# Output additions at later places, the layout transposes split by batch, and a prelude that starts its statistics two places later

## The chip, the cores and the metric

The kernel runs on one core of one Trainium2 chip. The metric is the device time of one execution in microseconds, as the median of several runs. TensorE is called PE here, its weight loads PEld, VectorE DVE, ScalarE ACT, GpSimd POOL and SyncE SP.

## The reference

Sixteen batches of 1024 nodes with 128 features go through two graph layers; `adj` is one 1024 × 1024 matrix, shared by all batches.

```python
h = relu(layernorm(x))
x = x + (adj @ (h @ weight) + bias)              # layer 0, per batch
h = relu(layernorm(x))                           # layer 1
for _ in range(5):
    m = adj @ h                                  # in_matrix and out_matrix are both adj
    av = concat([m, m])
    u3 = h @ u3_w.T + u3_b
    z = sigmoid(av @ w3_w.T + w3_b + u3)
    r = sigmoid(av @ w4_w.T + w4_b + u3)
    hv = tanh(av @ w5_w.T + w5_b + (r * h) @ u5_w.T + u5_b)
    h = (1 - z) * h + z * hv
x = x + h
```

## The kernel before

Batches are worked in eight pairs. Layer 1 is a chain of five steps for each pair, and two pairs are in work at a time: the even pair and the odd pair take turns, a step of one and then a step of the other. In this text "p_n" is step n of pair p, so the order is 0_0, 1_0, 0_1, 1_1, ... 0_4, 1_4, 2_0, 3_0 and so on to 7_4.

A step (`step`, L726) has an aggregate and gates. The aggregate (`aggregate`, L382) computes adj @ h for both batches by 26 products of 4 matmuls each (L400), whose right-hand sides are sums of blocks of adj, made once, and whose left-hand sides ("forms") are sums of blocks of h, made on DVE or copied by ACT. EARLY forms are made during the gates of the step before, LATE forms within the aggregate. ACT copies product banks out of PSUM (tu, vw, x, rs, d, g, yz, mn, j, kl, hi) and DVE adds them up into mT (L424, L427, called "sums" here; the last sums are P3, Q and P). The copies d, j share one buffer.

The gates (`gates`, L670) then go over four units (batch, half of the nodes), in the order batch 1, batch 1, batch 0, batch 0: first r of all units (matmuls pr, L690, L691), then z (L697), then for each unit the matmuls pv, tanh (L706), and three DVE operations that update hT (L708 to L710). hT is h with features on the partitions. The next aggregate of this pair wants h with nodes on the partitions ("natural", hN). `natural_from` (L552) makes it: DVE transposes 32 × 32 squares of hT (L558) into sq, sq is stored to DRAM (fn), and four loads per batch bring it back to hN with the blocks in place. All DMAs are issued on SP, in the order in which they are written.

Layer 0 and the normalizations of later pairs ("preludes", L604) run in the background of the steps. A prelude is a generator: it loads x of two batches, yields some times, and then does a piece at each call (statistics by bn_stats on DVE, `scales` on DVE and POOL, `shift` on DVE, Relu on ACT, and so on). It ends its first part with BLOCK, upon which its own aggregate (bT_a and so on) stands between two steps; whether this is so is looked up once per step, ahead of the gates. Its results are stored ("parked") and loaded back when the pair begins, as natural h (hP) and, by squares (sqt) that DVE transposes (L575), as hT.

Where the pieces stand is written out by hand. `place(k)` (L595) is called after product k of an aggregate (k from 1 to 26), and at r0 to r3 and z0 to z3 in the gates. It first runs what `put` has fixed there, and at places 7, 10, 17, 24, r1, r3 and z2 it also runs one piece of the background or, at some of these, one waiting output addition from `todo`. A pair's result is x + h; its four output additions (L823, two per batch) wait in `todo` after its last step and are run during the step that comes next. They read hN and the x (x1) that was loaded again.

The engines' programs are fixed in the order written, for every engine.

Of the kernel before, what the change touches and what calls it, by code (L numbers as in the profile page):

```python
# [8 lines left out]
F32 = mybir.dt.float32  # L9
# [4 lines left out]
P = 128  # L14
# [5 lines left out]
SQ = 32  # L20
NSQ = P // SQ
# [121 lines left out]
ANY, BLOCK, HOLD = range(3)  # L143
FREE = (7, 10, 17, 24)
PLAIN = ((0, 0), (1, 1), (0, 1), (1, 0))
UNITS = ((1, 0), (1, 1), (0, 0), (0, 1))
# [3 lines left out]
def tile_two_gnn_layers(  # L150
# [9 lines left out]
    nc = tc.nc  # L160
    pin = tc.keep_in_program_order
    B, N, D = x.shape
    NC = N // P
    NH = N // HALF
# [8 lines left out]
    flip = ctx.enter_context(tc.tile_pool(name="flip", bufs=2))  # L173
# [8 lines left out]
    def dma(out, in_):  # L182
        pin(nc.sync.dma_start(out=out, in_=in_))  # L183
# [351 lines left out]
    def scratch_for(kind, nm):  # L535

        scratch = dram.tile([P, N], F32, tag=f"{kind}_{nm}", name=f"{kind}_{nm}")
        return scratch, scratch.rearrange("(a y) (k f) -> k y a f", a=NSQ, k=NSQ)

    def by_blocks(hN, k):  # L540
        return hN[bass.ts(k, SQ)].rearrange("y a j e -> y a (j e)")

    def natural_tile(nm, tag="hN"):
        return nat.tile([P, NSQ, NC, SQ], F32, tag=tag, name=f"{tag}_{nm}")

    def squares_of_half(sq, g):
        return sq[:, :, bass.ts(g, CH), :].rearrange("p k j e -> p j k e")

    def transposed_half(hT, g):
        return hT[:, bass.ts(g, HALF)].rearrange("p (j k e) -> p j k e", j=CH, k=NSQ)  # L550

    def natural_from(hT, nm):  # L552

        stored = {}
        for i in (1, 0):
            sq = flip.tile([P, NSQ, NC, SQ], F32, tag="sq", name=f"sq_{nm}_{i}")
            for g in range(NH):
                pin(nc.vector.transpose(squares_of_half(sq, g), transposed_half(hT[i], g)))  # L558
            scratch, stored[i] = scratch_for("fn", f"{nm}_{i}")
            dma(scratch, sq.rearrange("p k j e -> p (k j e)"))  # L560
        hN = {}
        for i in (1, 0):
            hN[i] = natural_tile(f"{nm}_{i}")
            for k in range(NSQ):
                dma(by_blocks(hN[i], k), stored[i][k])
        return [hN[0], hN[1]]

    def transposed_from(scratch, nm):

# [14 lines left out]
    fixed = {}  # L584
    todo = []
# [6 lines left out]
    def put(k, *pieces):  # L592
        fixed.setdefault(k, []).extend(pieces)

    def place(k):  # L595
        for piece in fixed.pop(k, ()):
            piece()
        if k in FREE or k in ("r1", "r3", "z2"):
            if todo and k in (10, 17, 24, "z2"):
                todo.pop(0)()  # L600
            elif background["kind"] == ANY:
                proceed()

    def prelude(pair, kept=None):  # L604


        both = (2 * pair, 2 * pair + 1)
        for b in both:
            if b not in xts:
                xts[b] = load_x(b)  # L610
        xt = [xts.pop(b) for b in both]
        yield ANY
        yield ANY
        while pair % 2 == 0 and pair > 2 and pair - 2 not in begun:
            yield HOLD
        h0 = [natural_tile(f"a{b}", "hP") for b in both]
        if kept is not None:
            slots = [h.rearrange("p a j e -> p (a j e)").rearrange("p (j d) -> p j d", d=D) for h in h0]
            h0 = [s.rearrange("p j (a e) -> p a j e", e=SQ) for s in slots]

        def add_bias(i):
            for c in range(NC):
                pin(nc.gpsimd.tensor_add(xt[i][:, c, :], xt[i][:, c, :], gb))

        if kept is not None:
            bias_of[pair] = lambda: [add_bias(i) for i in range(2)]
        then = add_bias if kept is None else lambda i: None
        yield from normalize(h0, xt, f"a{pair}", then, in_halves=pair == 0)
        background["h"] = h0
        yield BLOCK  # L630
        if kept is not None:
            aT = aggregate_plainly(slots, f"a{pair}", place)
        else:
            aT = aggregate(h0, f"a{pair}", background["place"], spare=True)
        for i, g in PLAIN:
            yield ANY
            pt = ps_g.tile([P, CH, D], F32, tag="pg", name=f"po_{both[i]}_{g}")
            for j in range(CH):
                pin(
                    nc.tensor.matmul(  # L640
                        pt[:, j, :],
                        aT[i][:, bass.ts(g * CH + j, P)],
                        w_sb[:, WG, :],
                        start=True,
                        stop=True,
                    )
                )
            half = xt[i][:, bass.ts(g, CH), :]
            pin(nc.vector.tensor_add(half, pt, half))
        for i, b in enumerate(both):  # L650
            x1s[b] = dram.tile([P, NC, D], F32, tag=f"x1d_{b}", name=f"x1d_{b}")
        hN = [natural_tile(f"b{b}", "hP") for b in both]
        parked[pair] = []

        def park(i):
            scratch, blocks = scratch_for("ft", f"{both[i]}")
            for k in range(NSQ):
                dma(blocks[k], by_blocks(hN[i], k))
            dma(x1s[both[i]], xt[i])
            parked[pair].append((scratch, blocks))  # L660

        yield from normalize(hN, xt, f"b{pair}", park)
        if kept is not None:
            kept[pair] = hN
# [2 lines left out]
        for pair in range(first, pairs):  # L667
            yield from prelude(pair)

    def gates(mT, hT, nm):  # L670


        def view(t, u):
            return t[u[0]][:, bass.ts(u[1], HALF)]

        def add(bank, w, moving, start, stop):
            pin(
                nc.tensor.matmul(  # L678
                    bank, w_sb[:, w, :], moving, start=start, stop=stop, skip_group_check=True
                )  # L680
            )

        banks, rh, z = {}, {}, {}
        for k, u in enumerate(UNITS):
            tag = f"{nm}_{u[0]}{u[1]}"
            pg = ps_g.tile([P, HALF], F32, tag="pg", name=f"pr_{tag}")
            add(pg, W4A, view(mT, u), True, False)
            add(pg, U3, view(hT, u), False, True)
            r = work.tile([P, HALF], F32, tag="r", name=f"r_{tag}")
            pin(nc.scalar.activation(r, pg, AF.Sigmoid, bias=bsum[:, 1:2]))  # L690
            pin(nc.vector.tensor_mul(r, r, view(hT, u)))  # L691
            banks[u], rh[u] = pg, r
            place(f"r{k}")
        for k, u in enumerate(UNITS):
            add(banks[u], W3A, view(mT, u), False, True)
            t = work.tile([P, HALF], F32, tag="z", name=f"z_{nm}_{u[0]}{u[1]}")
            pin(nc.scalar.activation(t, banks[u], AF.Sigmoid, bias=bsum[:, 0:1]))  # L697
            z[u] = t
            place(f"z{k}")
        for u in UNITS:  # L700
            tag = f"{nm}_{u[0]}{u[1]}"
            pg = ps_g.tile([P, HALF], F32, tag="pg", name=f"pv_{tag}")
            add(pg, W5A, view(mT, u), True, False)
            add(pg, U5, rh[u], False, True)
            hv = work.tile([P, HALF], F32, tag="hv", name=f"hv_{tag}", bufs=3)
            pin(nc.scalar.activation(hv, pg, AF.Tanh, bias=bsum[:, 2:3]))  # L706
            h = view(hT, u)
            pin(nc.vector.tensor_sub(hv, hv, h))  # L708
            pin(nc.vector.tensor_mul(hv, hv, z[u]))  # L709
            pin(nc.vector.tensor_add(h, h, hv))  # L710


    state = {}
# [4 lines left out]
    def transposes(i, pair):  # L718

        both = {k: transposed_from(parked[pair][k][0], f"{2 * pair + k}") for k in (1, 0)}  # L720
        state[i]["next hT"] = [both[k][0] for k in range(2)]
        return both[1][1] + both[0][1]
# [3 lines left out]
    def step(i):  # L726
        st = state[i]
        pair, n = st["pair"], st["step"]
        nm = f"{pair}_{n}"
# [24 lines left out]
        if following is not None:  # L754
            for k, piece in zip(GATE_PLACES, make_forms(following, EARLY)):
                put(k, piece)
        gates(mT, hT, nm)
        if final:
            finish(pair, hT)
            st["pair"] = None  # L760
            return
        if last and not final:
            st["x1"] = [load_x1(2 * pair + k) for k in range(2)]
        for piece in fixed.pop("layout", ()):
            piece()
        hN = natural_from(hT, nm)
        st["step"] += 1
        st["hN"] = hN
        if last:
            for k in range(2):  # L770
                todo.extend(output(2 * pair + k, st["x1"][k], hN[k]))
# [13 lines left out]
    def load_x1(b):  # L785
        x1 = pre.tile([P, NC, D], F32, tag="xt", name=f"x1_{b}")
        dma(x1, x1s[b])
        return x1
# [43 lines left out]
    kept = {}  # L832
# [39 lines left out]

    def begin_second():
        begin(1, 1, kept[1])
        put("layout", *transposes(1, 1))
        background["gen"] = preludes(2)
        proceed()

# [53 lines left out]
```

## Time and profile before

| | |
|---|---|
| median of 3 runs | 1860.86 us (1859.23 to 1862.19) |
| profiled execution, its own time | 1861.88 us |
| its span | 1860.1 us |
| granted TensorE clock, mean | 0.998 |
| PE busy | 1825.0 us, 98% |
| DVE busy | 1386.9 us, 75% |
| ACT busy | 753.7 us, 41% |
| POOL busy | 122.8 us, 7% |
| DMA moved | 145.14 MB, mean 78 GB/s |

Times inside the profile are counted from the start of the span. "A <- B: t, n, m" in a list of waits says that A stood t us in total for B, n times, and m us the longest time. A row of windows gives the stretch, its length, the busy time of each engine with the number of instructions in parentheses, the granted clock, the DMA share and GB/s. A row of the timeline gives start, duration, engine, line, operation, what it writes and reads, and in brackets how long the engine stood idle before it and what ended that. Matmuls overlap by the profile's account, so that the time from one start to the next is shorter than a duration.

### The profile page before, as it was taken

The page shows a single profiled execution, that of the slowest core. Times are in us where ns is not written, and L with a number is a line of the kernel's source. Part 1 is how long each engine was busy: PE and PEld are TensorE (multiplying, and loading weights), DVE is VectorE, ACT ScalarE, POOL GpSimd, SP SyncE. Part 2 cuts the span into 40 slices and gives each one's busy share as a digit, 9 for nine tenths or more (in the row PEclk, how much of TensorE's full clock was granted, in tenths as well). Part 3 has the DMA queues.
Part 4 walks back from the last instruction along what each step waited for, and adds up shares of the span by engine and source line. Part 5 has one row for each costly group of instructions (what it writes and reads, how often), then busy time and mean ns, then how long its engine had stood idle before and what let it go on. Part 6 is the DMA issues. An engine that isn't in the chain of part 4 may idle for free.

```text
span 1860.1 us, 20599 instructions
## 1 busy us (share of the span) xinstructions
PE 1825.0 (98%) x6808; PEld 1269.9 (68%) x6808; DVE 1386.9 (75%) x3252; ACT 753.7 (41%) x1486; POOL 122.8 (7%) x168
## 2 busy tenths in 40 slices
PE   8999999999999999999999999999999999999998
PEld 4666876777766686677766668668766667766675
DVE  6787777777777787777777877778767777767775
ACT  3444344343334434434333532453433333334433
POOL 4211002000001000200000200020000000000000
PEclk9999999999999999999999999999999999999999
DMA  4231132104531113111542111311343312211123
GB/s 161 91 113 46 46 89 71 46 23 143 154 101 57 46 46 113 46 46 56 140 133 91 57 46 46 113 46 46 91 113 102 102 46 77 60 45 46 46 68 113
DMA packets 87514, 145.14 MB, mean 78 GB/s; under 512 B 9712, under 2 KB 64624, under 8 KB 87408
## 3 DMA queue, kind: packets, MB, share of 16 engines
q1 hardware_dynamic: 87408, 143.83, 26.1%
q8 instruction: 54, 0.88, 0.2%
q14 instruction: 52, 0.43, 0.1%
HBM read 77.73 MB, written 66.06 MB: 77 GB/s over the span
## 4 chain that ended last, share of the span: by engine, by line
PE 82%; DVE 7%; DMA 4%; ACT 3%; SPq 2%; issue 1%; POOL 0%; DVEq 0%; POOLq 0%; ACTq 0%
PE pr L678 20%; PE bT L400 17%; PE pv L678 14%; PE bV L400 8%; PE bX L400 5%; PE bT_a L400 3%; PE pq_a L519 3%; PE bD L400 3%; SPq L183 2%; PE bV_a L400 2%; PE po L640 1%; PE bF L400 1%; PE bJ L400 1%; PE bX_a L400 1%; DMA xt<-in_x_dram 1%
## 5 line engine op out<-in xcount | busy, mean ns | idle before, releaser
L400 PE MATMUL bT<-right_op,forms 128*128 128x256 f32 x1920 | 455.3, 379 | 4.1 <-ACT yz L412 3.5
L400 PEld LDWEIGHTS bT<-right_op,forms 128*128 128x128 f32 x1920 | 363.8, 190 | 69.9 <-issue 8.4
L678 PE MATMUL pr<-mT,w_sb 128*128 128x512 f32 x640 | 310.2, 597 | 14.4 <-DVE mT L427 14.4
L400 PE MATMUL bV<-right_op,forms 128*128 128x256 f32 x960 | 228.0, 379 | 0.0
L678 PEld LDWEIGHTS pr<-mT,w_sb 128*128 128x128 f32 x640 | 121.3, 191 | 155.2 <-issue 130.3
L691 DVE TENSOR_TENSOR r<-r,hT 128x512 f32<-128x512 f32 x160 | 111.8, 699 | 149.8 <-ACT r L690 148.0
L690 ACT ACTIVATE r<-pr,bsum 128x512 f32<-128x512 f32 x160 | 108.8, 685 | 273.5 <-PE pr L678 273.5
L400 PEld LDWEIGHTS bV<-right_op,forms 128*128 128x128 f32 x960 | 181.3, 190 | 24.1
L706 ACT ACTIVATE hv<-pv,bsum 128x512 f32<-128x512 f32 x160 | 109.3, 687 | 142.8 <-PE pv L678 142.6
L678 PE MATMUL pv<-mT,w_sb 128*128 128x512 f32 x320 | 164.3, 595 | 0.8 <-ACT z L697 0.8
L678 PE MATMUL pr<-hT,w_sb 128*128 128x512 f32 x320 | 165.0, 597 | 0.0
L708 DVE TENSOR_TENSOR hv<-hv,hT 128x512 f32<-128x512 f32 x160 | 109.9, 687 | 73.2 <-ACT hv L706 73.2
L678 PE MATMUL pv<-r,w_sb 128*128 128x512 f32 x320 | 163.4, 592 | 0.0
L400 PE MATMUL bX<-right_op,forms 128*128 128x256 f32 x640 | 157.7, 379 | 0.0
L400 PEld LDWEIGHTS bX<-right_op,forms 128*128 128x128 f32 x640 | 121.1, 190 | 16.2
L710 DVE TENSOR_TENSOR hT<-hT,hv 128x512 f32<-128x512 f32 x160 | 110.7, 692 | 17.0 <-DVE hv L709 0.5
L678 PEld LDWEIGHTS pv<-mT,w_sb 128*128 128x128 f32 x320 | 60.1, 190 | 80.5 <-issue 70.1
L709 DVE TENSOR_TENSOR hv<-hv,z 128x512 f32<-128x512 f32 x160 | 110.7, 692 | 5.5
L678 PEld LDWEIGHTS pr<-hT,w_sb 128*128 128x128 f32 x320 | 61.4, 192 | 77.6 <-issue 77.6
L697 ACT ACTIVATE z<-pr,bsum 128x512 f32<-128x512 f32 x160 | 107.8, 686 | 16.1 <-PE pr L678 16.1
L678 PEld LDWEIGHTS pv<-r,w_sb 128*128 128x128 f32 x320 | 60.8, 190 | 76.5 <-issue 56.7
L558 DVE STREAM_TRANSPOSE sq<-hT 128x512 f32<-128x512 f32 x156 | 96.8, 678 | 0.0
(168 smaller groups left out, 2258.2 us busy)
## 6 DMA issues: line engine op xcount, KB each, us to landing
fn<-sq SPq DMA_DIRECT2D x78, 512.0 KB, 2.7
hN<-fn SPq DMA_DIRECT2D x312, 128.0 KB, 3.4
ft<-hP_b SPq DMA_DIRECT2D x64, 128.0 KB, 2.6
x1d<-xt SPq DMA_DIRECT2D x16, 512.0 KB, 3.5
sqt<-ft SPq DMA_DIRECT2D x16, 512.0 KB, 5.7
x<-x1d SPq DMA_DIRECT2D x16, 512.0 KB, 5.2
xt<-in_x_dram SPq DMA_DIRECT2D x15, 512.0 KB, 6.5
out_dram<-x SPq DMA_DIRECT2D x14, 512.0 KB, 2.7
```

The costliest lines, as they stand in the source:

```text
L183: pin(nc.sync.dma_start(out=out, in_=in_))
L400: nc.tensor.matmul(halves(bank)[:, half], forms[:, FORM[form], c, :], right_op[:, RIGHT[name], c, :], start=bool(opens) and c == 0, stop=c ...
L519: nc.tensor.matmul(bank, hN[i][:, c, :], raw[c // SB][g][:, c % SB], start=c == 0, stop=c == NC - 1,)
L558: pin(nc.vector.transpose(squares_of_half(sq, g), transposed_half(hT[i], g)))
L678: nc.tensor.matmul(bank, w_sb[:, w, :], moving, start=start, stop=stop, skip_group_check=True)
L690: pin(nc.scalar.activation(r, pg, AF.Sigmoid, bias=bsum[:, 1:2]))
L691: pin(nc.vector.tensor_mul(r, r, view(hT, u)))
L697: pin(nc.scalar.activation(t, banks[u], AF.Sigmoid, bias=bsum[:, 0:1]))
L706: pin(nc.scalar.activation(hv, pg, AF.Tanh, bias=bsum[:, 2:3]))
L708: pin(nc.vector.tensor_sub(hv, hv, h))
L709: pin(nc.vector.tensor_mul(hv, hv, z[u]))
L710: pin(nc.vector.tensor_add(h, h, hv))
```

## The change

Four things are changed.

- The output additions stand at places 17, 24, r3 and z2 of the step in which they run; they stood at 10, 17, 24 and z2. Background pieces take the places that come free, and give up r3.
- `natural_from` is split. `squares_to_dram` (transposes and store of one batch) is called by `gates` through `then` as soon as the second unit of a batch is updated, so batch 1 is transposed and stored ahead of batch 0's update. The loads of hN follow after the gates, as before. In a pair's last step the loads of x1 are issued ahead of batch 1's store.
- A prelude that is not one of the first two yields four times instead of twice between its loads of x and its first piece.
- The four transposes that make pair 1's first hT are put at r0 to r3 of step 0_0; they stood behind the gates of that step, ahead of `natural_from`.

```diff
+    def squares_to_dram(hT, nm):
+        sq = flip.tile([P, NSQ, NC, SQ], F32, tag="sq", name=f"sq_{nm}")
+        for g in range(NH):
+            pin(nc.vector.transpose(squares_of_half(sq, g), transposed_half(hT, g)))
+        scratch, blocks = scratch_for("fn", nm)
+        dma(scratch, sq.rearrange("p k j e -> p (k j e)"))
+        return blocks
+
+    def natural_from(blocks, nm):
+        hN = natural_tile(nm)
+        for k in range(NSQ):
+            dma(by_blocks(hN, k), blocks[k])
+        return hN
...
-            if todo and k in (10, 17, 24, "z2"):
+            if todo and k in (17, 24, "r3", "z2"):
                 todo.pop(0)()
...
-        yield ANY
-        yield ANY
+        for _ in range(2 if kept is not None else 4):
+            yield ANY
...
-        for u in UNITS:
+        for k, u in enumerate(UNITS):
...
             pin(nc.vector.tensor_add(h, h, hv))
+            if k % NH == NH - 1:
+                then(u[0])
...
-        gates(mT, hT, nm)
+        stored = {}
+
+        def turn(k):
+            if final:
+                return
+            if last and k == 1:
+                st["x1"] = [load_x1(2 * pair + k) for k in range(2)]
+            stored[k] = squares_to_dram(hT[k], f"{nm}_{k}")
+
+        gates(mT, hT, nm, turn)
...
-        for piece in fixed.pop("layout", ()):
-            piece()
-        hN = natural_from(hT, nm)
+        hN = {k: natural_from(stored[k], f"{nm}_{k}") for k in (1, 0)}
...
-        put("layout", *transposes(1, 1))
+        for k, piece in zip(("r0", "r1", "r2", "r3"), transposes(1, 1)):
+            put(k, piece)
```

More of the change, by code (lines that the diff above doesn't have):

```diff
@@ L550, in transposed_half @@
         return hT[:, bass.ts(g, HALF)].rearrange("p (j k e) -> p j k e", j=CH, k=NSQ)
[L552 to L566, printed above, removed]
+    def squares_to_dram(hT, nm):
[10 more added lines that the diff above has]
+        return hN
     def transposed_from(scratch, nm):
@@ L668, in preludes, with gates @@
             yield from prelude(pair)
-    def gates(mT, hT, nm):
+    def gates(mT, hT, nm, then):
         def view(t, u):
@@ L761, in step @@
             return
-        if last and not final:
-            st["x1"] = [load_x1(2 * pair + k) for k in range(2)]
-        for piece in fixed.pop("layout", ()):
-            piece()
-        hN = natural_from(hT, nm)
+        hN = {k: natural_from(stored[k], f"{nm}_{k}") for k in (1, 0)}
         st["step"] += 1
-        st["hN"] = hN
+        st["hN"] = [hN[k] for k in range(2)]
         if last:
```

## The prediction

> **What bounds the kernel now.** I read the page first, then the waits of PE and of DVE, then windows cut at single steps, then the timeline around the gaps. [...]
>
> ```profile
> PE 1825.0 (98%) x6808; PEld 1269.9 (68%) x6808; DVE 1386.9 (75%) x3252; ACT 753.7 (41%) x1486; POOL 122.8 (7%) x168
> ...
> PE pr L678 <- DVE mT L427: 14.4, 11, 2.7
> PE pq_a L519 <- ACT hP_a L311: 6.7, 1, 6.7
> PE bF L400 <- ACT j L417: 5.5, 7, 1.6
> PE bT L400 <- ACT yz L412: 3.5, 3, 1.2
> ...
> DVE x L823 <- DMA hN<-fn: 32.0, 7, 5.2
> DVE stats_a L286 <- DMA xt<-in_x_dram: 13.7, 5, 3.4
> ```
>
> PE is the bound: 1825 of 1860.1 us. The change touches no matmul, so only PE's stalls can go. PE's own list names 31 us of them, and 6.7 of those are the start. The two DVE lines show where most of the rest comes from: DVE stood 7 times for hN, up to 5.2 us, and 5 times for a new x.
>
> ```profile
> 153.31:192.92 39.61, 39.61 (x145) 27.36 (x144) 28.50 (x59) 15.24 (x28) 0.00 (x0) 1.00 0.17 54
> 489.35:531.08 41.73, 40.04 (x145) 27.19 (x144) 32.88 (x67) 15.15 (x28) 0.00 (x0) 1.00 0.53 150
> 258.81:302.93 44.12, 41.45 (x145) 27.92 (x144) 33.11 (x83) 16.57 (x32) 1.65 (x1) 0.96 0.31 96
> 302.93:344.23 41.30, 40.14 (x145) 27.20 (x144) 31.62 (x74) 21.09 (x44) 10.35 (x17) 1.00 0.18 51
> 573.71:613.84 40.13, 39.88 (x145) 27.28 (x144) 32.69 (x87) 21.06 (x44) 11.65 (x18) 1.00 0.17 53
> ```
>
> Each row is one step with the same matmuls (columns: length, PE, PEld, DVE, ACT, POOL busy, clock, DMA share, GB/s). 39.61 us (step 0_1) is the step without a stall. The others are 1_4 (outputs inside; the window ends 0.11 short of the next step's start, 531.19), 0_2 (new x), 1_2 and 3_0 (parts of a prelude). What a step takes over 39.61 is its loss, hidden stretching of matmuls included.
>
> ```profile
> 504.81 0.69 DVE L823 TENSOR_TENSOR x<-x,hN 128x512 f32<-128x512 f32 x1 [4.28 <-DMA hN<-fn]
> 505.42 0.42 DVE L427 TENSOR_TENSOR mT<-d,rs 128x256 f32<-128x256 f32 x1
> ...
> 506.35 1.13 PE L400 MATMUL bF<-right_op,forms 128*128 128x256 f32 x4 [0.43 <-ACT j L417]
> 513.92 1.13 PE L678 MATMUL pr<-mT,w_sb 128*128 128x512 f32 x2 [1.25 <-DVE mT L427]
> ...
> 282.57 0.87 DVE L286 BATCH_NORM_STATS2 stats_a<-xt 128x6 f32<-128x128 f32 x4 [3.07 <-DMA xt<-in_x_dram]
> 284.09 2.08 PE L678 MATMUL pr<-mT,w_sb 128*128 128x512 f32 x2 [2.67 <-DVE mT L427]
> ```
>
> These are the mechanisms. In 1_4 the first output addition (place 10) stands 4.28 us for hN. Behind it in DVE's queue is mT<-d,rs; ACT's j copy reuses d's buffer, and bF's bank needs j. So PE stops 0.43, and the jammed DVE then ends the aggregate 1.25 late. In 0_2 the statistics at place 24 stand 3.07 us for x, ahead of the last mT sums, and the gates wait 2.67.
>
> [...] mT<-d,rs needs nothing of hN and yet starts 0.61 us after the addition. [...] after the gap of 2.67 us the first matmuls of 0_2 take 1.04 us on average (2.08 for two) where 0.59 is usual, and the window shows clock 0.96. After 2.0 us (step 2_2) it happened as well, after 1.41 (4_2) not. So the two long gaps cost 1.7 to 1.8 us beyond themselves.
>
> **The change part by part.** Step lengths are read from the timeline, first bT matmul to first bT matmul.
>
> 1. *Outputs at 17, 24, r3, z2 instead of 10, 17, 24, z2.* Seven steps hold outputs: 1_4, 2_0, 3_4, 4_0, 5_4, 6_0, 7_4. Their losses now: 2.23 + 2.91 + 2.52 + 2.01 + 3.17 + 1.88 + 2.16 = 16.9 us. When would hN be there? Its last block lands 15.3 to 16.6 us after the step's start (1_4: 504.62 − 489.35 = 15.27; worst 5_4: 16.56). In an undisturbed step (6_2, start 1609.56) DVE is through with place 17's sums at 1624.31, so +14.75. The wait left is 0.5 to 1.8 us before part 2. After it DVE has idle time to absorb it: 0.66 (for kl) + 0.29 (for bF) + 1.92 (for hi), less the 0.60 of the addition itself, so 2.2 us. Then the addition at 24 (0.60) comes behind the P3 sums (end +20.7 in 6_2) and makes the 0.69 us of the Q sum end at +22.0, and PE's 26 products end at +22.45. So it costs nothing. The addition moved to r3 lies in the gates: there DVE has, after the last r multiplication (ended 8.4 after the gates' start in 0_0), at most one transpose, six forms and two additions, 0.6 + 6 × 0.38 + 1.2 = 4.1 us, and is free at +12.5, when the first tanh of 0_0 ended at +12.9. PE reads none of that until the next step. Cover gone: 0.6 us × 7 = 4.2.
> 2. *Transpose and store behind each batch's update.* Nothing is added: still 156 transposes of 0.68 us (pitch 0.60), 78 stores, 312 loads. Batch 1's two transposes pass batch 0's six update operations, so batch 1's store is ready 4.3 us sooner (half of the 8.5 us that the twelve update operations took, 256.75 to 265.25) and batch 0's updates end 1.2 later; the last transpose ends as before, and so does all behind it on DVE. On SP, batch 0's store stands ahead of all hN loads and waits as before (6.78 after the start); batch 1's four loads then need not wait for a landing (7.2 instead of 8.27), but batch 0's four wait for their store's landing at 9.5. The last is issued at about 10.9 instead of 11.5: 0.6 us gained. This leaves 0 to 1.2 us at place 17. In last steps the x1 loads stand ahead of the first store on SP; in 1_4 the second waits for the output's landing and goes at 528.60, and the store will be ready near 532.4, so 3.5 us of margin.
> 3. *Four yields instead of two.* Statistics come two places later. In 0_2, 2_2 and 4_2 they go from 24 to r3, some 7 us later; the first x landed at 282.55, and DVE will be there at about 289. Losses now: 4.51 + 3.97 + 1.68 = 10.2 us, all gone. The odd preludes (pairs 3, 5, 7) miss the test ahead of the gates and run their aggregate one step later; that moves work, adds none, and their parked x is still read a step or more later.
> 4. *What it does to the places.* 1_2, 3_2 and 5_2 lose 1.69 each now: Relu groups at 7 and 10 hold ACT while yz's bank waits (the bT row of PE's list). They get exactly the pieces that 3_0 has now, which loses 40.13 − 39.61 = 0.52. Gain 3 × 1.17 = 3.5. 3_0 and 5_0 get their Relus one place later; unknown from −0.3 to +1.2 each (the 1_2 loss); I take 0. The six steps with a second prelude half keep 0.25 each.
> 5. *Layout transposes of pair 1 from after 0_0's update to r0–r3 of 0_0.* Now 1_0 loses 1.96 (2.4 us of transposes ahead of its sums); it gets the pieces that lose 0.25 in 1_1. Gain 1.7. At r0 DVE will stand about 1.9 us (it arrives at 97.8, sqt landed at 99.66), with r1 behind it; but PE needs r only from 106 on, so nothing; cover gone: 1.9 lost.
>
> Sum: 16.9 + 10.2 + 3.5 + 0 + 1.7 = 32.3 us. The profiled execution took 1861.88 (span 1860.1 and 1.8 around it), giving 1829.6. It stands 1.0 above the median of 1860.86; so **1829** for the median.
>
> **The rivals.**
> - *The wait only moves to place 17.* If hN comes no earlier, or DVE is too full to absorb 0.5 to 1.8 us, each of seven steps keeps about 1.1: 1829 + 7.7 = 1837. For it: DVE is busy 32.9 of 41.7 us in 1_4 and the DMA share is 0.53. Against: the idle time above.
> - *The shifted preludes jam ACT or DVE elsewhere.* Three steps keep 1.69, 3_0 and 5_0 grow to it: 3.5 + 2.3 = 5.8, so 1835. For it: the losses of 1_2 come from placement alone. Against: four of the arrangements already exist in the trace with 0.25 to 0.52.
> - *Slower: the transposes between updates hold PE.* If PE were to wait on batch 0's update or the ACT/DVE chain behind it, 39 steps lose up to 2 × 0.60 = 1.2 us: 46.8 − 32.3, so 1875. It turns slower once more than 0.83 us per step shows on PE. Against: in the clean step DVE is busy only 28.5 of 39.6, the next reader of that hT is a step of the same pair, 22 us off or more, and the total ahead of the next sums is unchanged.
> - *Nearly all stalls go*, the 0.25s too: 36.6 in all, 1824.
>
> **How the numbers follow.** Main case 0.70, wait at 17 0.13, shifted jam 0.08, all gone 0.04, slower 0.04, a wash 0.01. 0.2% (3.7 us) is what a measurement can tell from no change; all but the last two are faster by more: 0.95. The range runs from 1825.5 (part 4's unknown at its best, and most of the 0.25s) to 1838 (the first rival with a little added).
>
> **What would show it.** In the changed profile: x<-DMA hN<-fn falls from 32 us to under 6, stats_a<-DMA xt loses all but the start's part, PE's pr<-mT row falls from 14.4 to under 3, bF<-j and bT<-yz vanish, and the clock of 0_2 is 1.00. A step 1_4 above 40.5 us, or hv waiting in a way that PE's pv shows, would prove part 1 or 2 wrong.

## The result, and the profile after

The changed kernel takes 1832.09 us (median of 4 runs, 1831.76 to 1832.83) against 1860.58 for the kernel before on the same chip. The ratio is 0.9847, with a 95% interval of 0.983 to 0.9864: 28.5 us less. The forecast was 1829, with a range of 1825.5 to 1838. Of the profiled executions, which the sum of the prediction was made against, the times are 1861.88 before and 1831.96 after, and the spans 1860.1 and 1830.0: 30.1 us less, where the sum said 32.3.

The page's row of busy times of the changed kernel:

```profile
PE 1815.9 (99%) x6808; PEld 1270.2 (69%) x6808; DVE 1387.0 (76%) x3252; ACT 752.8 (41%) x1486; POOL 122.2 (7%) x168
```

PE's whole list of waits in it, and the rows of DVE's list that answer to those shown of before:

```profile
PE pq_a L519 <- ACT hP_a L311: 6.6, 1, 6.6
PE pv L679 <- ACT z L698: 3.2, 5, 1.3
PE bT L400 <- ACT hi L412: 0.4, 1, 0.4
...
DVE stats_a L286 <- DMA xt<-in_x_dram: 6.3, 2, 3.3
...
DVE x L831 <- DMA hN<-fn: 2.8, 3, 1.7
...
DVE hT L575 <- DMA sqt<-ft: 1.8, 1, 1.8
```

The rows PE pr <- mT (14.4 us), bF <- j (5.5) and bT <- yz (3.5) are gone. DVE's wait for hN fell from 32.0 to 2.8 us (3.1 with an addition that stood 0.3 us without a named releaser), and its waits for x are down to the two that belong to the start. The wait for sqt at r0 of step 0_0 (1.8 us) is new and was forecast. New too is the size of PE pv <- z: 3.2 us, where it was 0.8. PE's busy time fell by 9 us with the same matmuls: in the windows of the prediction they were busy for 40.04 us in 1_4 and 41.45 in 0_2 (granted clock 0.96), and below it is 39.61 in both.

The windows of the same four kinds of step as in the prediction (1_4, 0_2, 1_2, 3_0) show where the rest stands:

```profile
482.07:521.68 39.61, 39.61 (x145) 27.36 (x144) 33.10 (x67) 15.23 (x28) 0.00 (x0) 1.00 0.54 155
257.22:296.83 39.61, 39.61 (x145) 27.36 (x144) 31.80 (x70) 16.55 (x32) 0.00 (x0) 1.00 0.36 107
296.83:336.95 40.12, 39.88 (x145) 27.28 (x144) 32.69 (x87) 21.04 (x44) 11.64 (x18) 1.00 0.18 53
561.29:602.43 41.14, 39.89 (x146) 27.28 (x144) 32.27 (x89) 20.91 (x44) 11.50 (x18) 1.00 0.18 52
```

1_4 and 0_2 are at 39.61, the length of the step without a stall, and 0_2's clock is 1.00. 1_2 lost 1.69 and loses 0.51. 3_0 lost 0.52 and now loses 1.53: that is the forecast's miss. This table has the loss over an undisturbed step for every step that changed, each read from the timeline as in the prediction:

| steps | before | after |
|---|---|---|
| seven output steps | 16.9 | 0.0 |
| 0_2, 2_2, 4_2 | 10.2 | 0.0 |
| 1_2, 3_2, 5_2 | 5.1 | 1.5 |
| 1_0 | 1.96 | 0.25 |
| 0_1 | 0.00 | 0.32 |
| 3_0, 5_0 | 1.04 | 3.07 |

The sum falls by 35.2 − 5.2 = 30.0 us; the spans differ by 30.1. In 1_4 DVE's timeline reads thus:

```profile
496.49 0.42 DVE L427 TENSOR_TENSOR mT<-j,o 128x256 f32<-128x256 f32 x1
496.98 0.69 DVE L831 TENSOR_TENSOR x<-x,hN 128x512 f32<-128x512 f32 x1
497.59 0.42 DVE L424 TENSOR_TENSOR mT<-kl 128x256 f32<-128x256 f32 x1
```

The addition follows place 17's sums with no wait worth a bracket: hN's last block landed 14.72 us after the step's start and DVE got there at +14.83.

### The profile page after: what moved, and what is told of

It reads as the page before. It is cut to its first block, busy times and chain, and to the rows that moved or that the text cites. A ratio compares the mean times of both kernels' runs of the same rounds, so it can differ in the third digit from the quotient of the medians.

```text
span 1830.0 us, 20616 instructions
## 1 busy us (share of the span) xinstructions
PE 1815.9 (99%) x6808; PEld 1270.2 (69%) x6808; DVE 1387.0 (76%) x3252; ACT 752.8 (41%) x1486; POOL 122.2 (7%) x168
## 4 chain that ended last, share of the span: by engine, by line
PE 97%; ACT 1%; DVE 1%; issue 0%; DMA 0%; POOL 0%; ACTq 0%; DVEq 0%; POOLq 0%
PE bT L400 22%; PE pr L679 21%; PE pv L679 15%; PE bV L400 11%; PE bX L400 7%; PE bD L400 4%; PE bT_a L400 3%; PE pq_a L519 3%; PE bF L400 2%; PE bJ L400 2%; PE bV_a L400 2%; PE po L640 2%; PE bX_a L400 1%; ACT hP_a L311 1%; PE bD_a L400 1%; ACT r L691 0%
## 5 line engine op out<-in xcount | busy, mean ns | idle before, releaser
L556 DVE STREAM_TRANSPOSE sq<-hT 128x512 f32<-128x512 f32 x156 | 101.2, 687 | 0.0
```

## The experiments

e1 to e4 are built from the kernel before, and e5 to e8 and e10 from the changed one. e9 is the kernel before with other data. e1 to e4, e5 to e8, and e9 with e10 each shared a chip and the runs of the kernel before on it.

**One part alone: the outputs (e1).**

```diff
-            if todo and k in (10, 17, 24, "z2"):
+            if todo and k in (17, 24, "r3", "z2"):
```

> The kernel before with one edit: outputs at 17, 24, r3, z2. My theory (the seven output steps lose 16.9 us because the first addition stands for hN ahead of the sums, and at place 17 DVE has the idle time to absorb what is left of the wait): the seven steps fall to 39.61 us each, while 3_0 and 5_0 get the pieces of the changed kernel (shift and Relu at r3) and lose 1.52 instead of 0.52 each, so 1860.6 - 16.9 + 2.0 = 1845.7. Rival (the wait only moves to 17, since hN lands no earlier here): each of the seven keeps about 1.1, so 1853.4, with PE's pr row still fed by them.

Measured: 1847.47 us, ratio 0.9915 (0.990 to 0.993) to the kernel before beside it (1862.74). In the profile all seven output steps are at 39.61, and 3_0 and 5_0 lose 1.53 and 1.52. So this single line brings the 16.9 us and also the 2.0 lost in 3_0 and 5_0. hN's last block lands where it did (mean +15.64 against +15.68 before), and DVE stands for it 0.5 to 1.6 us at place 17 without PE noticing. The rival is out.

```profile
PE pr L678 <- DVE mT L427: 7.9, 4, 3.2
...
PE pv L678 <- ACT z L697: 2.9, 3, 1.3
...
DVE stats_a L286 <- DMA xt<-in_x_dram: 14.1, 5, 3.6
...
DVE x L823 <- DMA hN<-fn: 6.2, 7, 1.6
```

These rows of e1's lists of waits show it: DVE stands 7 times for hN, up to 1.6 us, yet pr <- mT is down to four waits: three for x, and one in step 1_0.

**One part alone: the yields (e2).**

```diff
-        yield ANY
-        yield ANY
+        for _ in range(2 if kept is not None else 4):
+            yield ANY
```

> The kernel before with one edit: four yields instead of two. My theory: the three waits for x go, with the slow clock behind two of them (10.2 us), and 1_2, 3_2 and 5_2 lose 0.51 instead of 1.69 (3.5 us): 1846.9; granted clock 1.00 in 0_2 and 2_2. Rival (only the waits' visible gaps of 2.67, 2.01 and 1.41 go, and the Relu stall of 1_2 moves along): 1860.6 - 6.1 = 1854.5.

Measured: 1848.54 us, ratio 0.992 (0.9905 to 0.9935), 14.2 us less. Its windows of 0_2 and 1_2:

```profile
259.16:298.77 39.61, 39.61 (x145) 27.36 (x144) 31.80 (x70) 16.57 (x32) 0.00 (x0) 1.00 0.34 107
298.77:338.90 40.13, 39.88 (x146) 27.28 (x145) 32.69 (x87) 21.06 (x44) 11.65 (x18) 1.00 0.17 53
```

0_2 is clean with the clock at 1.00, and 1_2 loses 0.52. My theory holds; the rival's 1854.5 is out. 3_0 and 5_0 keep their 0.52 here: their growth does not come from the yields.

**The layout alone, and layout with split (e3, e4).** The layout edit is the one of the change. The split can't stand without it: the layout transposes hold both buffers of sq until the gates are over, and the split needs one of them within the gates.

> The kernel before with one edit: pair 1's layout transposes at r0 to r3 of step 0_0. My theory: step 1_0 falls from 41.57 to about 40.13, the length of 3_0, whose pieces it shares: 1.4 us less, 1859.2. DVE stands about 1.9 us at r0 for sqt and PE does not notice. Rival (that stand reaches PE): 1861 or above, and 0_0's gates longer than 17.2.

Measured: 1858.62 us (median of 9), ratio 0.9983 (0.9972 to 0.9994), which is some 3 us, where I expected 1.4. The layout does not account for that: step 1_0 loses 1.07 instead of 1.96, where I expected 0.5. Of the 3.3 us between the spans of the two profiled executions, 2.3 stand in 2_2: its gap on PE was 1.41 us instead of 2.01, and the clock did not fall behind it (the granted clock of the whole execution is 0.999, where the kernel before has 0.998). Why that gap was shorter was not tested. DVE stands 2.2 us for sqt at r0, and 0_0's gates are 17.17 as before:

```profile
97.12 0.69 DVE L691 TENSOR_TENSOR r<-r,hT 128x512 f32<-128x512 f32 x1 [1.74 <-ACT r L690]
100.03 0.71 DVE L575 STREAM_TRANSPOSE hT<-sqt 128x512 f32<-128x512 f32 x1 [2.22 <-DMA sqt<-ft]
```

So the wait at r0 is real and hidden, as forecast.

> The kernel before with two edits: the layout transposes as in the run beside it, and each batch transposed and stored right behind its update (the buffers of sq allow the second only with the first). Against the layout alone. My theory: hN lands 0.4 to 0.6 us earlier in the seven output steps, which still stand for it at place 10, and their loss follows nearly one to one: 7 x 0.45 = 3.1 us less, so 1859.2 - 3.1 = 1856.1. Rival (the transposes between the updates hold PE): slower, up to 39 x 1.2 = 47 us. Second rival (the loss does not follow the landing): no difference, 1859.2.

Measured: 1855.45 us, ratio 0.9954 (0.994 to 0.9969), 3.2 us below e3. The number is as expected, but the profile does not show it coming by my way: the seven output steps lose 16.3 us in all against e3's 17.0, and hN's last block lands at a mean of +15.59 against +15.69. Most of the difference between the two profiled executions stands in 0_2, which loses 2.36 instead of 4.37: PE's gap was 2.10 us instead of 2.40, and the clock did not fall behind it (granted clock 1.00 from 258 to 300 us). So the agreement of the number is luck, and how much of the 3.2 us the split itself earns stays open. What is settled is that transposes between the updates do not hold PE: the slower rival is out.

**The change without the split (e5).**

> The changed kernel without the split by batch: both batches are transposed and stored behind the gates. My theory: hN lands 0.4 us later in the output steps, DVE's wait at 17 grows from 0 to 1.7 us by as much, and its idle time of about 2.2 us absorbs it: no difference to the changed kernel, 1832.1. Rival (the split carries part of the gain): the seven steps lose up to 0.4 each, 1835.

Measured: 1832.04 us (ratio to the kernel before 0.9851, 0.9836 to 0.9865) against 1832.09 of the changed kernel; its losses are the same step for step within 0.07 us. hN's last block lands at a mean of +15.61 instead of +15.24, and DVE stands 6.0 us in all ahead of the first additions instead of 3.1 (4.4 and 2.8 of it put down to hN, the rest to no releaser), with the output steps at 39.61 all the same. In the changed kernel the split brings nothing that can be measured.

**Is it the place or the wait? (e9)** The kernel before, in which the output is 2x because each addition takes x twice:

```diff
-                pin(nc.vector.tensor_add(part, part, h[:, :, js, :]))
+                pin(nc.vector.tensor_add(part, part, part))
```

> The kernel before with its outputs still at 10, 17, 24 and z2, but each addition adds x to itself instead of h, so it needs no hN (the output is 2x there; same DVE operations, DMAs and places). My theory: the wait is what costs, not the place. With three additions and no wait the Q sum of an output step ends at 20.7 + 0.6 + 0.69 = +22.0, as the idle 2.87 us ahead of hi takes in the first two; PE ends at +22.45, so the seven steps lose nothing: 1860.6 - 16.9 = 1843.7, with 3_0 and 5_0 at 0.52. Rival (the three additions ahead of the gates fill DVE, wait or no wait): the steps keep about 1.07, the gap that all seven share ahead of pr, so 1851.

Measured: 1843.25 us, ratio 0.9894 (0.9874 to 0.9913), with all seven output steps at 39.61 within 0.01 and 3_0, 5_0 at 0.51. So three additions at 10, 17 and 24 cost nothing, and the 16.9 us were the wait for hN alone.

**How long may the wait be? (e10)** The changed kernel with the first addition at 14:

```diff
-            if todo and k in (17, 24, "r3", "z2"):
+            if todo and k in (14, 24, "r3", "z2"):
```

(and 14 is let in as a place for outputs.)

> The changed kernel with the first output addition at 14 instead of 17. DVE gets there at about +13.2 and stands until hN lands, +14.7 to +15.4 in six steps and about +16.9 in 5_4. My theory (DVE has 2.87 us idle behind it, and a step loses 20.7 + (wait + 0.6 - 2.87) + 0.6 + 0.69 - 22.45 if that is above nothing): waits of 1.5 to 2.3 cost nothing, 5_4's 3.7 costs about 1.0: 1833.1. Rival (every wait of DVE ahead of the last sums shows on PE): 7 x about 1.9 = 13 us more, 1845.

Measured: 1832.88 us, ratio 0.9839 (0.9816 to 0.9861); its other steps are as in the changed kernel. DVE stood 1.5 to 2.2 us in six of the steps, and they lose nothing. In 5_4:

```profile
1400.30 0.69 DVE L831 TENSOR_TENSOR x<-x,hN 128x512 f32<-128x512 f32 x1 [3.26 <-DMA hN<-fn]
...
1406.55 1.13 PE L679 MATMUL pr<-mT,w_sb 128*128 128x512 f32 x2 [0.51 <-DVE mT L427]
```

It stood 3.26 us and loses 0.78: 0.67 up to its gates, 0.51 of that as a gap on PE, and 0.10 in them. With 3.26 the formula of the expectation gives 20.7 + (3.26 + 0.6 − 2.87) + 0.6 + 0.69 − 22.45 = 0.53, against the 0.67. The same formula, with 4.28 us and two additions ahead of the P3 sums, gives 20.7 + (4.28 + 1.2 − 2.87) + 0.6 + 0.69 − 22.45 = 2.15 for 1_4 of the kernel before, which lost 2.12 up to its gates. In all seven output steps of that kernel it is within 0.23 us of what they lost up to their gates (1.78 to 3.06).

**The miss: 3_0 and 5_0 (e6, e7, e8).** In the changed kernel an output addition holds r3 in 2_0 and 4_0, so that pairs 4 and 6 run one piece fewer there, and in 3_0 and 5_0 shift and Relu of the second batch fall on r3. ACT's timeline in 3_0, and PE's behind it:

```profile
593.19 1.65 ACT L311 ACTIVATE hP_a<-xt,nmr_a,rstd_a 128x128 f32<-128x128 f32 x4 [1.69 <-DVE nmr_a L303]
594.74 1.81 ACT L698 ACTIVATE z<-pr,bsum 128x512 f32<-128x512 f32 x3
...
595.46 1.13 PE L679 MATMUL pv<-mT,w_sb 128*128 128x512 f32 x2 [1.25 <-ACT z L698]
```

ACT stands 1.69 us for nmr, then does four Relus, and the first z comes behind them, though its matmuls are long done. pv needs the bank that z reads, and PE stands 1.25 us. e6 gives r3 back to the background:

```diff
-            if todo and k in (17, 24, "r3", "z2"):
+            if todo and k in (17, 24, "z0", "z2"):
```

(and z0 is let in as a place for outputs.)

> The changed kernel with the third output addition at z0 instead of r3, so that the background keeps r3 and pairs 4 and 6 get their pieces in steps 2_0, 3_0, 4_0 and 5_0 as in the kernel before. My theory (the 1.52 us that 3_0 and 5_0 lose each come from shift and Relu at r3, where ACT stands for nmr ahead of z): they fall back to 0.52 each, 2.0 us less, 1830.1. Rival (they come from POOL's bias additions, which lie in the same gates and beside which DVE's forms take 0.67 instead of 0.42 us): the bias additions stay in those gates or close by, so no difference, 1832.1.

Measured: 1830.02 us, ratio 0.9841 (0.9826 to 0.9855); 2.0 us under e5 beside it. 3_0 and 5_0 lose 0.51 each. POOL is as busy in its 3_0 as in that of the changed kernel (11.66 us in the window against 11.50), so it is the order of the pieces that this edit mends: the shift stands at r1 again, ahead of the last two r.

> The changed kernel with the outputs at 24, r1, r3, z2 (none at 17): then no piece of pairs 4 and 6 is run in 2_0 and 4_0, and 3_0 and 5_0 get the order of 1_0 (Relu of the first batch at r1 and r3, shift and Relu of the second at z2). My theory: they lose 0.25 each instead of 1.52, 2.5 us less, 1829.6; the wait for hN is gone altogether. Rival (r1 is too full with an addition, and r reaches pv late): the seven output steps lose 0.2 to 0.6 each, 1831 to 1834.

The tuple of places is (24, "r1", "r3", "z2"). Measured: 1830.45 us, ratio 0.9843 (0.9828 to 0.9857). 3_0 and 5_0 lose 0.26 each, as expected, and the output steps nothing, so the rival is out; but 2_1 and 4_1, which have the last Relus of pairs 4 and 6 at place 7 now, lose 0.32 and 0.31. That I had not counted; 0_1 of the changed kernel loses 0.32 in the same way.

> The changed kernel without the bias additions of layer 0 for pairs 2 to 7 (96 POOL operations left out), so the output lacks that bias there. My theory (shift and Relu at r3): 3_0 and 5_0 still lose 1.2 to 1.5 us each, 1831.5 to 1832.1. Rival (POOL slows DVE's forms there, and so delays nmr and all behind it): they lose 0.5 or less, 1830 or under, and DVE's forms in those gates take 0.42 us again.

Measured: 1830.20 us, ratio 0.984 (0.9823 to 0.9856), 1.8 us under e5. 3_0 and 5_0 lose 1.00 each: less than my theory allowed, more than the rival. 0_1 loses 0.00 instead of 0.32, and 1_2, 3_2 and 5_2 lose 0.26 instead of 0.51. Two of DVE's groups in the gates of 3_0 in the changed kernel, with 16 POOL additions in those gates (the number ahead of the last bar is the mean of one in ns):

```profile
L374 DVE TENSOR_TENSOR forms<-hN 128x256 f32<-128x256 f32 x3 | 1.8, 590 | 0.0
...
L303 DVE SCALAR_TENSOR_TENSOR nmr_a<-mv_a,rstd_a 128x8 f32<-128x8 f32 x1 | 0.4, 413 | 0.0
```

The same two groups in e8, without those additions:

```profile
L374 DVE TENSOR_TENSOR forms<-hN 128x256 f32<-128x256 f32 x3 | 1.3, 419 | 0.0
...
L303 DVE SCALAR_TENSOR_TENSOR nmr_a<-mv_a,rstd_a 128x8 f32<-128x8 f32 x1 | 0.2, 159 | 0.0
```

With POOL at work a form takes 590 ns on average instead of 419, and nmr 413 instead of 159. ACT's stand for nmr falls from 1.69 to 1.17 us. So of the 1.53 us in 3_0, POOL's additions bring 0.53. e6, which mends the order of the pieces, takes away 1.02 with POOL left in. The 0.51 that stays in e6 is in part POOL's as well: 1_2, which has the same pieces there, falls from 0.51 to 0.26 without the additions. So the two causes overlap; both mended at once was not run.

e6 has the lowest median of the study, 0.4 us below e7. It is 2.0 us below e5, the equal of the changed kernel, and 1.6% below the kernel before.

## Why the prediction was right

Its time was 3 us too low, inside its range, and its main case came about. By its own parts:

1. *Outputs, 16.9 us:* right in size, 0.0 left. The wait that was to remain at 17 (0 to 1.2 us) was 0 to 1.7, and the idle time took it. e1 shows the part alone, e9 that the wait was its whole cause, e10 how long a wait may be.
2. *Split, 0 us by itself:* right; e5 shows it. The forecast of hN 0.6 us earlier was large: on average it is 0.44 against the kernel before, 0.37 against e5, and 0.10 in e4 against e3. Batch 0's store, issued at the same moment, landed at +9.76 instead of +9.51 in 1_4, and batch 0's loads are issued only after it. Why it landed later was not tested.
3. *Yields, 10.2 us:* right against the execution it was read from, the slow clock behind two of the waits included; e2 shows that the waits and the slow clock go. The size holds for that execution alone: with the yields left as they were, 0_2, 2_2 and 4_2 lose 11.0 us in e1, 9.1 in e9, 7.7 in e3 and 5.6 in e4, as the gaps differ and the clock falls behind some of them only. The prediction reads 1.04 us for a matmul at the slow clock (0.50) off two that overlap (2.08); the same reading of two usual ones is 1.02 for both, so that a factor of two stands.
4. *Places:* 3.5 us in 1_2, 3_2 and 5_2 were right (3.54). **The step that was mis-sized is "3_0 and 5_0 get their Relus one place later ... I take 0".** They cost 1.01 and 1.02 us more, near the upper end of 1.2 that was kept for it. I looked at how many Relus fall in the gates, not at what stands between them on ACT: a shift at r3 makes ACT wait for DVE ahead of z. The arrangement of 1_1, which was the nearest in the trace, has its shift at z2, behind three of the z. e6 puts it right with 2.0 us.
5. *Layout, 1.7 us in 1_0:* right in the whole change (1.71); alone it brought 0.9 (e3), since 1_0 keeps its old pieces there (the yields alone take 0.4 off it in e2). The stand at r0, put at 1.9 us, was 1.8 and hidden. Not in the sum was 0_1, which got a Relu group at place 7 and loses 0.32. With e8, where it loses 0.00, this turns out to come from POOL's bias additions, which now run beside DVE's updates of the gates ahead: twelve of them from 146.24 to 153.29, and the five update operations that start from 149.57 to 153.01 take 0.76 to 0.94 us, where they took 0.68 or 0.69 in the kernel before.

Together: 32.3 − 2.0 − 0.3 = 30.0, and the spans differ by 30.1. That is 2.3 us of the 3 by which the time was too low. The rest is the 1.0 us that the prediction took off to get from the profiled execution to the median: the profiled execution of the changed kernel (1831.96) does not stand above its median (1832.09), so there was nothing to take off. So the medians differ by 28.5 only.

## What to carry to other kernels

Where a kernel has many equal stages, take the shortest as the measure and read each stage's loss from it: this finds the stretching of matmuls that the list of waits hides (PE busy 41.45 us in 0_2 for the work of 39.61), and it let this sum come out within 2.3 us. A DMA wait of DVE cost nothing here as long as it fitted into DVE's idle time ahead of the next thing that PE needed: in e10, with 2.87 us idle, waits of 1.5 to 2.2 us were free and one of 3.26 us cost 0.78. Work out that time, which here gave the losses within 0.23 us, and put the waiting operation behind the urgent ones. When pieces of background work move, look at what each engine's queue has right behind them: a piece that waits for another engine must not stand ahead of work that releases the bound engine (in 3_0 ACT stood 1.69 us for nmr ahead of z, and PE 1.25 us for z).

## What the runs showed of the hardware

- *The matmul clock fell behind some PE gaps of 2.0 to 3.2 us and not behind others, and the two kinds differ in where the gap lies.* It fell behind gaps of 2.01 and 2.67 us (before), 3.23 (e1), 2.40 (e3) and 2.77 us (e9); it did not behind 2.34 (e1), 2.10 (e4) and 2.25 us (e9), nor behind any of 1.74 or less. In the kernel before the clock stands at 0.50 for 3.41 us from 283.87 and again from 744.67; the two falls begin 460.80 us, or 135 × 3.413, apart. So I cut each execution into stretches of 3.413 us counted from a fall. The first two rows are such stretches of the kernel before around its gap of 2.01 us, the last two of e1 around its gap of 2.34 us (134 stretches behind its fall at 283.44):

```profile
741.26:744.67 3.41, 1.40 (x6) 0.74 (x5) 2.06 (x6) 0.00 (x0) 0.00 (x0) 1.00 0.17 71
744.67:748.08 3.41, 3.41 (x5) 1.37 (x5) 0.24 (x1) 0.96 (x3) 0.00 (x0) 0.50 0.03 5
...
737.41:740.83 3.42, 1.99 (x10) 1.41 (x8) 0.69 (x5) 0.00 (x0) 0.00 (x0) 1.00 0.48 193
740.83:744.24 3.41, 2.50 (x6) 1.25 (x7) 1.45 (x4) 0.48 (x1) 0.00 (x0) 1.00 0.03 6
```

The gap of 2.01 us lies in one stretch, and the clock is halved for the next; the gap of 2.34 us is split by a border, 1.42 and 0.91 us, and the clock stays. The other gaps agree: PE idled 2.01 to 2.45 us in the stretch ahead of each of the five falls, and at most 1.55 in any other stretch of the steps (the 2.25 us of e9 are split as 0.96 and 1.29; the 2.10 us of e4, which has no fall, as 0.60 and 1.49, counted from the rise of its clock at the start). Each fall cost 1.5 to 3.0 us in the gates behind it (gates of 18.75 to 20.24 us instead of 17.27); it lasted one stretch, in e1 two. A stretch in which PE idled 2.01 of its 3.41 us was enough here. That the idle time within a stretch decides is my reading of these five falls; no run moved a gap across a border to test it.
- *DVE was slower beside POOL's additions.* Three forms of 128x256 take 419 ns on average without and 590 in gates with 16 POOL additions of 128x128 (e8 against the changed kernel), and nmr takes 159 and 413. By what means the additions do this was not tested.
